# When four scatter accumulators are zeroed: a graph-network layer on one Trainium2 core

## The chip, the cores and the metric

The kernel runs on one core of one Trainium2 chip. The metric is the time of one execution on the device in microseconds (us). The kernel before takes 2061.96 us, the median of three runs (2057.36 to 2062.47).

A core has five engines that this text names as the profile does: PE (matrix products; PEld is its weight load), DVE (vector work), ACT (activations and copies), POOL and SP. SP does no arithmetic here: it issues almost all the plain transfers, in program order, and an entry in its queue that waits for a semaphore holds up every entry behind it. POOL issues the indirect transfers (the scatters).

## The reference, cut to what matters

A graph has 6250 nodes with 128 features and 200000 edges. Every edge takes the row of its `dst` node, multiplies it by a filter worked out from 20 edge attributes, and the result is added to the row of its `src` node.

```python
h = relu(layernorm(x))
v = h @ W_in
W_ij = (softplus(f_ij @ W_f1 + b_f1) - log 2) @ W_f2 + b_f2
W_ij = W_ij * f_ij_cutoff
x_ij = v[dst] * W_ij
out  = segment_sum(x_ij, src, num_segments=6250)
y    = x + (softplus(out @ W_o1 + b_o1) - log 2) @ W_o2 + b_o2
```

The edges are sorted by `dst`; `src` is in no order. The segment sum over `src` is the part that this change touches.

## The kernel before, in words

**Tiling.** 128 edges are a chunk, four chunks a quad; 391 quads. A loop over items `i` (L1208) works on several quads at once: in item `i`, PE makes the first product of quad `i+1` (`s1_pe`, L313), gathers and filters quad `i-1` (`s2_pe_x`, `s2_pe_w`), DVE multiplies the two (`s2_m`, L520), and so on. In the middle of the run an item takes a little under 5 us. What stands beside this skeleton is hung into it by `at(item, point, function, ...)`; `run(i, point)` calls it. The point "L" is the first of an item, right behind the loads of two coming quads (`load_sc`, in even items, for the quads four and five ahead). Nothing is reordered afterwards: each engine runs its instructions in the order in which the functions are called.

**Two ways for the segment sum.** 168 of the quads (`mpq`, from quad 8 on, every second or third one) are permuted on chip and summed by PE into `accT`, an SBUF tile of 128 x 6272 numbers. The other 223 quads (`splain`) are scattered by POOL: `scatter` (L579) adds 128 rows of 512 bytes to an accumulator in DRAM, one instruction per chunk. Rows that overflow on the first way are scattered as well (`os`, `oji` in the profile). In all there are 987 scatters.

**Accumulators.** An addition to a row reads it and writes it back, so two scatters that may touch the same rows must not be under way together: a scatter waits until the last one into the same accumulator has landed. There are four accumulators of 6400 rows (`ACC_R`), `acc0` to `acc3`, and `acc_of` (L566) picks one by the scatter's number `k`: `acc0` alone up to `K1_END`, `k % 2` up to `K2_END`, `k % 3` up to `K3_END`, then `k % 4`, and near the end the last three. Each has to be zeroed before its first use, by ten pieces (`zero_piece`, L164) of 320 KB that copy a zeroed stretch `zero` of `accT` into DRAM. POOL issues the pieces of `acc0` and `acc1` in the first 40 us, SP those of `acc2` (items `Z2`) and `acc3` (items `Z3`).

**Lists.** Within a chunk, edges with the same `src` must be summed before the scatter. 31 of the scattered quads do this on PE (`s3_pe`; the index tile is `ji`). The other 192, quads 12 to 203 of `splain`, form 12 windows of 16 quads: one edge of each chunk and node goes to the node's row, duplicates go to rows of a list behind the 6400 rows (index tile `lji`, worked out by `l_eq` to `l_index` during the window before, from `sb` loads two items earlier). The list of window `w` has 128 rows from `l_base(w)` on, and later windows have lower ones: a scatter of window `w` is allowed the rows up to `l_base(w) + 128`, its own list and those of the later windows. When a window is done, `l_load` (`lm` in the profile) reads its 128 list rows from the four accumulators and they are added to their nodes. The list rows of all windows, 1536 in each accumulator, are zeroed by three pieces of 256 KB per accumulator (`zero_list`, L170), in items 1 to 12.

**Buffers.** The data of a scatter lies in one of four `s` buffers per quad, which comes free when the scatters that read it have landed. The index tile `oji` has two buffers.

Of the kernel before, what the change touches and what calls it, by code (L numbers as in the profile page):

```python
# [7 lines left out]
F32 = mybir.dt.float32  # L8
# [12 lines left out]
P = 128  # L21
# [13 lines left out]
SW = 16  # L35
# [19 lines left out]
def tile_gnn(ctx: ExitStack, tc: tile.TileContext, x, fB, cT, srcT, srcr, dstr, win_, wf1, wf2, bias, bo1c, wo1,  # L55
             wo2, consts, ident, cmap, out, n_edges):
    nc = tc.nc
    N = out.shape[0]
    NP = x.shape[0]
# [15 lines left out]
    ACC_R = NP + P  # L75
    GN = NP // GRP
    ZR = 10 if ACC_R % 10 == 0 else 1
    ZL = 3
    K1_END, K2_END, K3_END = 2, 8, 140
    Z2, Z3 = [0,0,1,1,2,2,3,3,4,4], [5+2*j for j in range(10)]  # L80
    mpq = sorted_quads(NQ)
    mpi = {q: n for n, q in enumerate(mpq)}
    units = unit_its(mpq)
    splain = [q for q in range(NQ) if q not in mpi]
    plain = {q: n for n, q in enumerate(splain)}
    NS = len(splain)
    LB, LE = listed(NS) if spread else (0, 0)
# [6 lines left out]
    NW = (LE - LB) // SW  # L94
    LR = P * NW
# [8 lines left out]
    cp = ctx.enter_context(tc.tile_pool(name="cp", bufs=1))  # L104
# [7 lines left out]
    accs = []  # L112
# [25 lines left out]
    wo1_sb = cp.tile([P, P], F32, name="wo1_sb")  # L138
    wo2_sb = cp.tile([P, P], F32, name="wo2_sb")
    accT = cp.tile([P, NP], F32, name="accT")  # L140
    zero = accT[:, :ACC_R // ZR]
    wgtb = cp.tile([P, 1], BF16, name="wgtb")
    iotw = cp.tile([P, GN // 2 + SLOTS], F16, name="iot")
    iot = iotw[:, GN // 2:]
# [22 lines left out]
        for h in range(parts):  # L167
            eng.dma_start(v[j][:, h * w:(h + 1) * w], zero[:, :w])

    def zero_list(k, j):  # L170
        v = accs[k][ACC_R:].rearrange("(p t) f -> p (t f)", p=P)
        w = LR // ZL
        nc.sync.dma_start(v[:, j * w:(j + 1) * w], zero[:, :w])

    def xt_load(g):
        o, T = groups[g]
# [186 lines left out]
    def l_base(w):  # L363
        return ACC_R + P * (NW - 1 - w)
# [470 lines left out]

    with tc.manual_schedule():
        nc.scalar.preload_act_table_set("natural_log_exp_and_others")
        nc.gpsimd.memset(zero, 0.0)
        for j in range(ZR * 4 // 10):
            zero_piece(nc.gpsimd, 0, j)  # L840
# [108 lines left out]
        def at(i, point, fn, *a):  # L949
            hooks.setdefault((i, point), []).append((fn, a))  # L950
# [6 lines left out]
        if CE < EP // P:  # L957
            w = (CE + 4 * NS) // 2
# [128 lines left out]
        if spread:  # L1087
            k = clear(mid + 9, busy, 2)
# [3 lines left out]
            k = clear(NQ - 1, busy, 2)  # L1092
# [21 lines left out]
        for r in range(-(-len(mpq) // RKQ)):  # L1114
            i = mpq[RKQ * r]
            at(i - 5, "D2", rank_group, r)
            k = clear(i - 4, units)
            at(k, "PE2", rank_count, r)
            at(k + 1, "D0", rank_own, r)
            k = clear(k + 1, units)  # L1120
# [5 lines left out]
        for w in range((LE - LB) // SW):  # L1126
# [25 lines left out]
            k = clear(i + 1, units)  # L1152
# [5 lines left out]
            at(k + 2, "S", over_scatter, ("L", w))  # L1158
        if LE:
            for k in range(NACC):  # L1160
                for j in range(ZL):
                    at((0, 3, 6, 9)[k] + j + 1, "L", zero_list, k, j)
        for q in mpq:
            at(q + 1, "D2", perm_oh, q)
            at(q + 2, "D2", part_rem, q, 1)
# [17 lines left out]
            if mpi[q] % 2 or q == mpq[-1]:  # L1183
                at(q + 5, "DM", over_idx, q)
                at(q + 6, "A0", over_dg, q)
                k = clear(q + 6, units)
                at(k, "PE2", over_row, q)
                at(k + 1, "D0", over_eq, q)
                k = clear(q + 8, units)
# [259 lines left out]
def sorted_quads(nq):  # L1449
    qs, q = [], MP0  # L1450
    while q < nq - MPEND:
        qs.append(q)
        q += MPGAPS[(len(qs) - 1) % len(MPGAPS)]
    return qs if len(qs) % RND <= EXTRA else qs[:len(qs) // RND * RND]
# [14 lines left out]
def listed(ns):  # L1469
    k = (ns - LEARLY - LLATE) // SW  # L1470
    b = (ns - LLATE - SW * k) // 4 * 4
    return b, b + SW * k
# [6 lines left out]
def clear(i, busy, n=1):  # L1479
    while any(i + k in busy for k in range(n)):  # L1480
        i += 1
    return i
# [113 lines left out]
```

## Time and profile before

| | |
|---|---|
| median of three runs | 2061.96 us |
| the profiled execution, time | 2079.2 us |
| the profiled execution, span of its instructions | 2077.4 us |
| mean granted clock of PE | 0.963 |
| bytes moved by DMA | 272.57 MB, mean 131 GB/s |
| scatters on POOL | 987, mean 1.62 us |

Times in the profile's rows are us from the start of the span. A timeline row has the start, the duration, the engine (with a "q" for an instruction that only issues a transfer), the source line, the operation, "out<-in" by the program's names, the shape, "xcount" for rows merged, and in brackets the idle time of the engine before it and what ended it. "DMA acc<-s,ji" as what ended it means the landing of a scatter. A row of the groups has "busy us, mean ns" behind the first bar and "idle us" with its releasers behind the second. A row of the waits reads: who waited, for whom, us in total, times, longest.

### The profile page before, as it was taken

The numbers are of one execution on the slowest core, as the hardware profiler recorded it, in microseconds if no ns is written. First come the engines' busy times: TensorE is split into PE (matmuls) and PEld (weight loads), VectorE is DVE, ScalarE is ACT, GpSimd is POOL, SyncE is SP. The second block draws the span as 40 slices with busy tenths as digits, with TensorE's granted clock in tenths as the row PEclk, the third lists the DMA queues.
The fourth block names the chain that finished last, engine by engine and source line by source line (L and its number), as shares of the span: only waits on it lengthen the run. The fifth ranks groups of instructions, "written<-read, shape, count | busy, mean of one in ns | idle before, by whom it ended". The sixth has DMA issues, their size and how long they took to land. (4 is left out here: it accounts for less than half of the span.)

```text
span 2077.4 us, 57578 instructions
## 1 busy us (share of the span) xinstructions
PE 1862.5 (90%) x20381; PEld 1288.0 (62%) x20381; DVE 1659.4 (80%) x4448; ACT 1482.8 (71%) x4083; POOL 1643.9 (79%) x1040
## 2 busy tenths in 40 slices
PE   3579988899999999999999999999999999999956
PEld 2456666566666666666666666666666666677734
DVE  3678887797888888988988978979889788787635
ACT  2468776777776777777678777777877777788714
POOL 3578787888877888887878878888888888888774
PEclk9679999999999999999999999999999999999977
DMA  7887766667766766766667666676676676667648
GB/s 238 227 210 147 125 118 120 121 112 130 130 118 114 126 127 119 139 123 123 120 120 130 120 119 118 118 124 117 120 134 108 124 121 111 110 119 131 130 48 239
DMA packets 381188, 272.57 MB, mean 131 GB/s; under 512 B 97727, under 2 KB 341354, under 8 KB 380898
## 3 DMA queue, kind: packets, MB, share of 16 engines
q0 software_dynamic: 143728, 71.30, 35.2%
q1 hardware_dynamic: 236882, 197.50, 34.1%
q8 instruction: 161, 2.64, 0.5%
q14 instruction: 129, 1.06, 0.2%
q10 hardware_dynamic: 288, 0.07, 0.0%
HBM read 154.45 MB, written 114.24 MB: 129 GB/s over the span
## 5 line engine op out<-in xcount | busy, mean ns | idle before, releaser
L582 POOL DMA_INDIRECT acc<-s,lji x768 | 1245.7, 1622 | 266.6 <-issue 180.3
L687 PE MATMUL pq<-pt,pm 128*128 128x387 bf16 x2688 | 533.0, 341 | 44.6 <-DVE pt L676 10.6
L510 ACT ACTIVATE xc<-xg,cb 128x128 f32<-128x128 f32 x1564 | 446.4, 371 | 135.7 <-PE xg L497 119.9
L505 PE MATMUL W<-w,a 128*128 128x128 f32 x3128 | 464.1, 292 | 0.1
L505 PEld LDWEIGHTS W<-w,a 128*128 128x128 f32 x3128 | 388.4, 195 | 42.3 <-issue 3.1
L687 PEld LDWEIGHTS <-pm 128*128 128x128 bf16 x2688 | 260.3, 99 | 233.4 <-issue 37.2
L693 ACT CAST mst<-pq 128x387 bf16<-128x387 f32 x672 | 302.2, 481 | 135.0 <-PE pq L687 96.5
L781 PE MATMUL un<-so,mst 32*128 32x392 bf16 x8064 | 374.5, 327 | 17.3 <-DVE pr L627 7.0
L781 PEld LDWEIGHTS <-mst 32*128 32x128 bf16 x8064 | 227.8, 93 | 157.1 <-issue 60.2
L323 ACT ACTIVATE a<-a,con 128x512 f32<-128x512 f32 x391 | 282.3, 722 | 12.7
L582 POOL DMA_INDIRECT acc<-s,ji x123 | 200.2, 1628 | 80.4 <-issue 26.4
L318 ACT ACTIVATE a<-z 128x512 f32<-128x512 f32 x391 | 238.3, 610 | 26.8 <-PE z L313 17.2
L676 DVE TENSOR_TENSOR pt<-pt 128x512 f32<-128x512 f32 x336 | 231.8, 690 | 5.8
L662 DVE TENSOR_SCALAR pm<-iot,pos 128x576 bf16<-128x576 f16 x672 | 221.8, 391 | 0.0
L792 DVE TENSOR_TENSOR accT<-un,accT 128x392 f32<-128x392 f32 x320 | 158.6, 558 | 73.7 <-PE un L781 37.5
L520 DVE TENSOR_TENSOR s<-W,xc 128x512 f32<-128x512 f32 x192 | 131.9, 687 | 85.9 <-ACT xc L510 52.0
L766 DVE TENSOR_SCALAR so<-iot,mst 128x392 bf16<-128x392 f16 x672 | 191.0, 344 | 6.7 <-PE un L781 6.7
L582 POOL DMA_INDIRECT acc<-os,oji x96 | 156.4, 1629 | 31.2 <-issue 18.0
L497 PE MATMUL xg<-wn,oh 63*128 63x128 bf16 x1564 | 157.3, 222 | 15.8 <-ACT xc L510 9.4
L313 PE MATMUL z<-ft,ws 123*128 123x512 bf16 x391 | 152.0, 389 | 15.7 <-DVE iotl L941 9.4
L494 PE MATMUL W<-b2rep,onesb 64*128 64x512 bf16 x391 | 153.9, 394 | 0.0
L520 DVE TENSOR_TENSOR pt<-W,xc 128x512 f32<-128x512 f32 x168 | 115.2, 686 | 47.9 <-ACT xc L510 29.5
(209 smaller groups left out, 2435.5 us busy)
## 6 DMA issues: line engine op xcount, KB each, us to landing
rb<-reld SPq DMA_DIRECT2D x391, 64.0 KB
fsd<-f SPq DMA_DIRECT2D x49, 480.0 KB
ft<-fsd SPq DMA_DIRECT2D x195, 120.0 KB
sb<-src SPq DMA_DIRECT2D x169, 128.0 KB
fb<-in_fB_dram SPq DMA_DIRECT2D x49, 320.0 KB
ft<-fsd SPq DMA_DIRECT2D x195, 80.0 KB
wn<-tab SPq DMA_DIRECT2D x782, 15.8 KB
acc<-s,lji POOLq DMA_INDIRECT x768
```

The costliest lines, as they stand in the source:

```text
L318: nc.scalar.activation(a, st[q]["z"], AF.Exp)
L323: nc.scalar.activation(a, a, AF.Ln, bias=half, scale=0.5)
L505: nc.tensor.matmul(W[:, c, :], st[q]["a"][:, c * P:(c + 1) * P], w2, start=False, stop=(c == 3))
L510: nc.scalar.mul(xc[:, c, :], st[q]["xg"][:, c, :], late["c", q // CQ][:, 4 * (q % CQ) + c:4 * (q % CQ) + c + 1])
L520: nc.vector.tensor_tensor(m[:, :, :P], st[q]["W"], st[q]["xc"], op=ALU.mult)
L582: nc.gpsimd.indirect_dma_start(out=accs[k][:rows, :], out_offset=bass.IndirectOffsetOnAxis(ap=ji, axis=0), in_=s, in_offset=None, compute_ ...
L662: nc.vector.tensor_scalar(pm[:, c], iot[:, :SLOTS], rk[r]["pos"][:, 4 * j + c:4 * j + c + 1], None, op0=ALU.is_equal)
L676: nc.vector.tensor_tensor(pt[:, :, k * P:(k + 1) * P], a, high(a), op=ALU.subtract)
L687: nc.tensor.matmul(t[:, :PW], mp[q]["pm"][:, c, s * P:(s + 1) * P], high(mp[q]["pt"][:, c:c + 1, :PW])[:, 0], start=(c == 0), stop=(c == 3))
L693: nc.scalar.copy(mp[q]["ms", s][:, :PW], mp[q].pop(("q", s))[:, :PW])
L766: nc.vector.tensor_scalar(so, iotw[:, :GN], w[:, 3 * P // 2:3 * P // 2 + 1], None, op0=ALU.is_equal)
L781: nc.tensor.matmul(ts[g][:, :GN], mp[q]["ms", s][v, k * P:(k + 1) * P], mp[q]["oh"][v], start=(q == qs[0] and k == 0), stop=(q == qs[-1] a ...
```

## The change

The third accumulator comes into use with scatter 40 (before: 8); it is zeroed in items 6 to 15 (before: 0 to 4), the fourth in items 20 to 38, every second one (before: 5 to 23, every second one). The tile `zero` moves to the last 640 columns of `accT`. The list rows are zeroed by 48 pieces of 64 KB (128 rows of 512 bytes, one per window and accumulator) out of a zeroed tile `zl` of its own; the four of a window stand 8, 6, 4 and 2 items ahead of the window's first quad. The descriptor space of POOL's transfers is set to 8192 bytes of a partition (before: the default, 16384). The instructions of PE, DVE and ACT and their order are the same as before; POOL has one memset more, SP 36 transfers more.

```diff
-    ZL = 3
-    K1_END, K2_END, K3_END = 2, 8, 140
-    Z2, Z3 = [0,0,1,1,2,2,3,3,4,4], [5+2*j for j in range(10)]
+    K1_END, K2_END, K3_END = 2, 40, 140
+    Z2, Z3 = [6 + j for j in range(10)], [20 + 2 * j for j in range(10)]
...
-    zero = accT[:, :ACC_R // ZR]
+    zero = accT[:, NP - ACC_R // ZR:]
+    zl = cp.tile([P, P], F32, name="zl")
...
-    def zero_list(k, j):
-        v = accs[k][ACC_R:].rearrange("(p t) f -> p (t f)", p=P)
-        w = LR // ZL
-        nc.sync.dma_start(v[:, j * w:(j + 1) * w], zero[:, :w])
+    def zero_list(k, w):
+        o = l_base(w)
+        nc.sync.dma_start(accs[k][o:o + P, :], zl)
...
+        nc.gpsimd.memset(zl, 0.0)
         nc.gpsimd.memset(zero, 0.0)
...
         if LE:
             for k in range(NACC):
-                for j in range(ZL):
-                    at((0, 3, 6, 9)[k] + j + 1, "L", zero_list, k, j)
+                for w in range(NW):
+                    at(max(1, splain[LB + SW * w] - 8 + 2 * k), "L", zero_list, k, w)
...
-    nc = bacc.Bacc("TRN2", target_bir_lowering=False, num_devices=1)
+    nc = bacc.Bacc("TRN2", target_bir_lowering=False, num_devices=1, dynamic_dma_scratch_size=8192)
```

## The prediction

> **What bounds the kernel now.** I read the page first, for the busy shares, the slices and the chain of waits; then the groups of POOL by stretch of time, its timeline, the waits, and last SP's, DVE's and ACT's timelines around the places where the new transfers will stand.
>
> ```profile
> PE 1862.5 (90%) x20381; PEld 1288.0 (62%) x20381; DVE 1659.4 (80%) x4448; ACT 1482.8 (71%) x4083; POOL 1643.9 (79%) x1040
> ...
> PE   3579988899999999999999999999999999999956
> ...
> GB/s 238 227 210 147 125 118 120 121 112 130 130 118 114 126 127 119 139 123 123 120 120 130 120 119 118 118 124 117 120 134 108 124 121 111 110 119 131 130 48 239
> ...
> PE 31%; DVE 6%; ACT 3%; DMA 3%; issue 2%; POOL 2%; SPq 1%; DVEq 0%; POOLq 0%; ACTq 0%
> ```
>
> A slice is 52 us. PE is full from the seventh slice on, and the chain, which reaches back over the second half of the span, runs mostly through PE. The first three slices are different: PE at 3, 5 and 7 tenths while DMA moves 210 to 238 GB/s, nearly twice the later 120. The next rows group POOL's scatters in three stretches (busy us, mean ns, then idle us and what ended it): 81 to 156, 156 to 376 and 1400 to 1800 us.
>
> ```profile
> L582 POOL DMA_INDIRECT acc<-s,ji x33 | 57.3, 1736 | 20.3 <-DMA acc<-s,ji 10.4 <-issue 5.4 <-ACT a L323 2.7
> ...
> L582 POOL DMA_INDIRECT acc<-s,lji x94 | 150.3, 1599 | 34.7 <-issue 20.4 <-DMA acc<-s,lji 7.2 <-DVE eql L369 1.6
> ...
> L582 POOL DMA_INDIRECT acc<-s,lji x187 | 302.9, 1620 | 57.0 <-issue 45.5 <-DMA acc<-s,lji 4.3 <-DVE accT L792 1.2
> ```
>
> A scatter costs POOL 1.6 to 1.7 us and about 0.3 us of issue. From 81 us on POOL hardly rests: (57.3+20.3)/33 = 2.35 us a scatter in the first stretch, with half of the idle time spent on the landing of an earlier scatter into the same accumulator, and (150.3+34.7)/94 = 1.97 us in the second. That POOL sets the pace of PE's side there, and not the other way, is seen in who waits for its landings:
>
> ```profile
> ACT s L540 <- DMA acc<-s,ji: 6.1, 3, 3.3
> ...
> 368.41 0.29 ACT L755 ACTIVATE oji<-ojd,con 128x1 int32<-128x1 f32 x1 [14.47 <-DMA acc<-os,oji]
> ```
>
> The first row (waits, 80 to 170 us) is ACT kept from refilling the four `s` buffers, the second is ACT standing 14.47 us until POOL had worked off its backlog. So a delay of POOL before 376 us is passed on whole: ACT resumes when POOL has caught up. Behind that, PE sets the pace.
>
> **The change, part by part.** The sum is made against the profiled execution's own 2079.2 us (span 2077.4), which is 17 above the median of the runs, 2061.96; I carry the difference over to that median.
>
> *Scatters 8 to 39 on two accumulators instead of three.* A scatter may start when the last one into its accumulator has landed. While `K2_END` was not reached, the trace already has two in use:
>
> ```profile
> 55.36 1.78 POOL L582 DMA_INDIRECT acc<-s,ji  x1 [18.73 <-ACT ji L563]
> 59.14 1.57 POOL L582 DMA_INDIRECT acc<-s,ji  x1 [2.00 <-DMA acc<-s,ji]
> 66.92 1.54 POOL L582 DMA_INDIRECT acc<-s,ji  x1 [6.21 <-DMA acc<-s,ji]
> ...
> 72.41 1.54 POOL L582 DMA_INDIRECT acc<-s,ji  x1 [2.04 <-DMA acc<-s,ji]
> ...
> 76.58 1.54 POOL L582 DMA_INDIRECT acc<-s,ji  x1 [0.30 <-DMA acc<-s,ji]
> ...
> 83.10 1.54 POOL L582 DMA_INDIRECT acc<-s,ji  x1 [0.65 <-DMA acc<-s,ji]
> ```
>
> All six go into accumulator 0, so the distances are start to restart: 3.78, 7.78, 5.49, 4.17, and 6.52 us once three are in use. With two accumulators the distance from scatter to scatter is half a restart, or 1.85 if that is more. I take 5.4 us, near the middle row: 2.7 us a scatter against 2.35, over 32 scatters +11. The ends are 2.1 (restart 4.2, -8) and 3.5 (restart 7, +37). That the restarts stay long has a reason in the change: zeroing is mostly moved within this stretch. Items 6 to 15 now issue ten pieces of the third accumulator (ten of 320 KB); before, six of the fourth's pieces and eight list pieces of 256 KB stood in items 5 to 15, about 4 MB against 3.5.
>
> The Trainium skill, "DMA: Bandwidth & Descriptors", section "Queues, rings and completion order", says that each DMA engine takes turns between the queues at packet granularity; by it a scatter's landing stretches whenever SP's queue has packets, so equal bytes would mean equal restarts. The trace bears it out as far as the row 66.92, with its wait of 6.21 us, lies where DMA moves 227 GB/s.
>
> *Items 0 to 5 lose their zeroing.* Ten pieces of the third accumulator and four list pieces, 4.3 MB, leave the stretch from 46 to 77 us. DVE's wait in the next row is for a load that stood in SP's queue behind such pieces:
>
> ```profile
> 46.30 0.97 SPq L168 DMA_DIRECT2D acc<-accT  x2
> 47.31 0.45 SPq L344 DMA_DIRECT2D sb<-src  x1
> ...
> 83.62 1.23 DVE L369 TENSOR_TENSOR eql<-sb,srcT_sb 128x1024 bf16<-128x1024 int16 x1 [8.76 <-DMA sb<-src]
> ```
>
> PE's side may come out of this up to 8.76 us earlier, but POOL is the bound, and for it only scatters 0 to 7 come sooner: between 0 and 6 us (the wait before 66.92), I take 3. Early part together: +8.
>
> *List pieces that wait.* Formerly all list rows were zeroed before any list scatter. Now the pieces of window w >= 1 are issued 8, 6, 4 and 2 items ahead of it, while scatters of window w-1 run, whose allowed rows include them. So each of 44 pieces waits on SP for the last list scatter into its accumulator, and the next one waits for the piece. Behind it in SP's queue stand the loads of the next items and the `sb` loads that DVE needs one or two items later. The price depends on how far POOL trails. Window 1, item 37 (SP, then POOL, then DVE):
>
> ```profile
> 243.00 3.06 SPq L295 DMA_DIRECT2D ft<-fsd  x3
> ...
> 250.13 0.84 SPq L344 DMA_DIRECT2D sb<-src  x2
> ...
> 259.10 2.14 POOL L582 DMA_INDIRECT acc<-s,lji  x1 [2.06 <-DMA acc<-s,lji]
> ...
> 256.56 1.21 DVE L369 TENSOR_TENSOR eql<-sb,srcT_sb 128x1024 bf16<-128x1024 int16 x1
> ```
>
> The piece stands ahead of 243.00 and must wait for the scatter of 259.10 to land, some 4 us later (3.78 was the shortest restart, 1.85x3 = 5.6 the turn that three accumulators allow). SP goes on at 263; it issues the item's loads and `sb` by 271 (7.1 us, as 243.00 to 250.13), landed at 274: DVE loses 17 us. POOL trails by about as much there, and the 14.47 us that ACT loses at 354 to 368 go away with its lead, so +3 (0 to 8).
>
> Window 11, item 325, has no such cover later:
>
> ```profile
> 1663.96 2.23 SPq L295 DMA_DIRECT2D ft<-fsd  x3
> ...
> 1670.69 1.79 SPq L344 DMA_DIRECT2D sb<-src  x4
> ...
> 1674.65 1.80 POOL L582 DMA_INDIRECT acc<-s,lji  x1 [0.31 <-issue]
> ...
> 1678.77 1.21 DVE L369 TENSOR_TENSOR eql<-sb,srcT_sb 128x1024 bf16<-128x1024 int16 x1
> ```
>
> Release at 1678.7, `sb` landed near 1688: 9 us on PE's path, of which POOL's backlog lets me count +8 (4 to 9). In window 6 (item 181) the same sum gives +3:
>
> ```profile
> 967.67 1.16 SPq L295 DMA_DIRECT2D ft<-fsd  x3
> ...
> 971.59 1.54 POOL L582 DMA_INDIRECT acc<-s,lji  x1 [0.30 <-issue]
> ...
> 974.01 0.85 SPq L344 DMA_DIRECT2D sb<-src  x2
> ...
> 981.36 1.21 DVE L369 TENSOR_TENSOR eql<-sb,srcT_sb 128x1024 bf16<-128x1024 int16 x1
> ```
>
> Release 975.6, `sb` issued 982 and landed at 984.5. In the other windows the scatter in question lands within a few us of SP's turn: 0 each, at most 5.
>
> *POOL behind the pieces.* A piece has the size of the lm loads, whose four issues at 778.6 to 779.9 us feed PE at 783.1:
>
> ```profile
> L469 PEld LDWEIGHTS lsum<-lm,leq x8: 192/192/192, 783.1 to 783.9; 128*128 128x128 f32 x8
> ...
> L451 SPq DMA_DIRECT2D lm<-acc x4: 355/380/382, 778.6 to 779.9; - x4
> ```
>
> 3.2 us after a landing at 4 makes 7.2. Three accumulators come round in 5.6 us (window 1: 1.6 each, twice), four in 7.4 (0 unless late). +2 (0 to 10).
>
> The Trainium skill, same page, section "Rules for kernel authors", advises to coalesce small transfers, since under 64 KB one pays mostly overhead; 48 pieces for 12 goes against it. On the estimate of 2 us fixed (that page, "Anatomy of one DMA") 36 more would cost 72 us if they stood one after the other on the path. The trace has the 3.2 us, but SP's queue runs ahead of its users, so I count only what is waited for.
>
> *The rest at nothing.* POOL's extra memset is a fifth of the one of `zero`; the zero tile at the end of `accT` is written only in item 42, after the last piece of item 38. The descriptor space is halved; if POOL had to wait for room, its scatters would last longer, and they keep a shortest time of 1.54 us in crowded and calm rows alike. Bound: the mean's excess, 1.62-1.54, over 987 scatters is 80 us, doubled at worst +80; I take 0.
>
> Sum: 8+3+8+3+2 = +24, 2103 in a profile, 2086 by the median; I say 2085.
>
> **The rivals.**
>
> *Faster: the landings get short.* If, with items 0 to 5 unloaded, a restart is 3.7 us or less, two accumulators cost nothing: 32 scatters at 2.05 instead of 2.35, -10, 3 earlier, and with a smaller backlog only half of the SP stalls, +7: 2056. For it: 3.78 and 4.17 do occur. Against: 5.49 to 7.78 too, at the same traffic that the change keeps in items 6 to 15. It decides below a restart of 3.7.
>
> *No change.* Restart 4.6 (2.3 a scatter, -2, and 3 earlier), and the late `sb` loads are absorbed by POOL's backlog in window 11 as in window 1: 2062. Against it: the chain is PE's there.
>
> *Much slower.* Restarts of 7 us all through (+37, 3 earlier), SP stalls +16: 2112. For it: 7.78 and 6.52. Against it: 2.35 x 3 = 7.05 is the most that three accumulators in turn allow, and only a third of those scatters waited.
>
> *The halved descriptor space makes POOL slower*, which isn't what the change is about: +80, 2142. Nothing shows it.
>
> **How the numbers follow.** Forecast 0.55 (its own range 2070 to 2100), faster 0.14, no change 0.11, much slower 0.16, descriptor space 0.04. The time is the forecast's, 2085. The range, 2058 to 2112, leaves out half of the faster case, the last one and the far half of the much slower one. A measurement here tells 0.3%, 6 us, from no change: slower 0.53+0.16+0.04+0.02 = 0.75, same 0.12, faster 0.13.
>
> **What would show it.** In the stretch of scatters 8 to 39: about 2.7 us each, with the landing of an earlier scatter as main releaser; below 2.2 the early term is wrong. At items 37 and 325: SP waiting some 15 to 20 us in the new list line, and DVE's `eql` waiting for `sb` right behind; if `eql` doesn't wait, those terms are wrong. ACT's 14.47 us before `oji` shrinks or goes. POOL's mean scatter stays near 1.62 us; if it grows, it was the descriptor space. A kernel whose first 156 us are shorter by 10 would overturn the forecast.

## The result, and the profile after

The changed kernel takes 2097.97 us (median of 5 runs, 2095.76 to 2100.06) where the kernel before takes 2062.47 (5 runs): the ratio is 1.0172, with the interval 1.0155 to 1.019. It is 35.5 us slower.

The page of the changed kernel begins with the busy shares, two rows of the 40 slices (52 us each) and the chain.

```profile
span 2095.7 us, 57684 instructions
PE 1863.1 (89%) x20381; PEld 1289.1 (62%) x20381; DVE 1655.6 (79%) x4448; ACT 1488.5 (71%) x4083; POOL 1629.0 (78%) x1041
...
PE   3578959999999999999899999999998989999956
...
GB/s 233 181 153 136 139 112 129 131 134 111 132 127 115 133 120 132 135 124 114 121 135 125 115 133 124 120 123 122 130 109 127 127 114 107 118 117 125 133 45 241
...
SPq 1%; DMA 1%; PE 0%; DVE 0%; ACT 0%; POOL 0%; issue 0%; DVEq 0%; POOLq 0%
```

PE is busy for 1863.1 us, where the two profiles of before (the second is that of experiment 1) have 1862.5 and 1855.9, so of the 35 us some 28 are idle time, and up to 7 may be slower work. The mean granted clock of PE is 0.957, against 0.963 and 0.965; from 200 to 300 us, where PE stands, it is 0.88 against 0.98 and 0.97. No run separates the clock from the waits. Slice 6 (262 to 314 us) has PE at 5 tenths where it had 8. The third slice moves 153 GB/s where it moved 210: the unloading of the start did happen. The chain reaches back over the end of the span only, so I read the groups and timelines. POOL's scatters, in the three stretches that the prediction used (busy us, mean ns, then idle us and what ended it):

```profile
L581 POOL DMA_INDIRECT acc<-s,ji x27 | 43.4, 1608 | 32.3 <-DMA acc<-s,ji 25.3 <-issue 6.6 <-ACT h L223 0.3
...
L581 POOL DMA_INDIRECT acc<-s,lji x89 | 142.4, 1600 | 36.1 <-issue 23.0 <-DMA acc<-s,lji 6.9 <-DVE s L519 1.3
...
L581 POOL DMA_INDIRECT acc<-s,lji x186 | 299.0, 1608 | 61.5 <-issue 43.0 <-DMA acc<-zl 5.4 <-DMA acc<-s,lji 4.6
```

From 81 to 156 us a scatter now takes (43.4+32.3)/27 = 2.80 us, and 25.3 of the 32.3 idle us end with the landing of an earlier scatter. A scatter itself costs POOL 1.61 us at 1400 to 1800 us, as before. How the early loss reaches PE's side is seen in ACT, which fills the `s` buffers that the landings free. These are its waits over the whole span, in the changed kernel and then in the second profile of before:

```profile
ACT s L539 <- DMA acc<-s,ji: 47.7, 8, 10.9
...
ACT s L540 <- DMA acc<-s,ji: 9.7, 2, 8.3
```

Then the two places that the prediction named. Item 37 (SP, then DVE and PE, and ACT's next `oji` behind):

```profile
253.16 0.46 SPq L264 DMA_DIRECT2D fb<-in_fB_dram  x1
273.37 0.32 SPq L172 DMA_DIRECT2D acc<-zl  x1
273.78 1.16 SPq L294 DMA_DIRECT2D ft<-fsd  x3
...
279.38 0.93 SPq L343 DMA_DIRECT2D sb<-src  x2
...
284.16 1.23 DVE L368 TENSOR_TENSOR eql<-sb,srcT_sb 128x1024 bf16<-128x1024 int16 x1 [17.90 <-DMA sb<-src]
285.31 0.69 DVE L519 TENSOR_TENSOR pt<-W,xc 128x512 f32<-128x512 f32 x1
...
286.05 0.58 PE L312 MATMUL z<-ft,ws 123*128 123x512 bf16 x1 [15.87 <-DMA ft<-fsd]
...
378.06 0.29 ACT L754 ACTIVATE oji<-ojd,con 128x1 int32<-128x1 f32 x1
```

SP issues nothing between 253.6 and 273.4, because the list piece waits; the `sb` loads stand behind it and `eql` loses 17.90 us. PE stands 15.87 us there. The row names a load of `ft` as what ended it, but that load was issued from 273.78 on, and `z` starts just as DVE's product behind `eql` ends (285.31 + 0.69 = 286.00); by the code, `z` takes the PSUM buffer that this product frees. So I read PE's wait as that of `eql`. The 14.47 us that ACT lost in front of `oji` are gone. Item 325:

```profile
1688.92 0.35 SPq L172 DMA_DIRECT2D acc<-zl  x1
1689.37 1.18 SPq L294 DMA_DIRECT2D ft<-fsd  x3
...
1694.65 3.19 SPq L343 DMA_DIRECT2D sb<-src  x4
...
1698.63 1.25 DVE L368 TENSOR_TENSOR eql<-sb,srcT_sb 128x1024 bf16<-128x1024 int16 x1 [7.88 <-DMA sb<-src]
```

The waits over the whole span (us, times, longest) put a number on the new line:

```profile
SPq L172 <- DMA acc<-s,lji: 126.4, 30, 19.7
...
DVE eql L368 <- DMA sb<-src: 37.8, 7, 17.9
...
POOL acc L581 <- DMA acc<-zl: 16.4, 20, 3.0
```

### The profile page after: what moved, and what is told of

Read it like the earlier page. It is cut to its first block, busy times and chain, and to the rows that moved or that the text cites. A ratio compares the mean times of both kernels' runs of the same rounds, so it can differ in the third digit from the quotient of the medians.

```text
span 2095.7 us, 57684 instructions
## 1 busy us (share of the span) xinstructions
PE 1863.1 (89%) x20381; PEld 1289.1 (62%) x20381; DVE 1655.6 (79%) x4448; ACT 1488.5 (71%) x4083; POOL 1629.0 (78%) x1041
## 5 line engine op out<-in xcount | busy, mean ns | idle before, releaser
L780 PE MATMUL un<-so,mst 32*128 32x392 bf16 x8064 | 381.4, 333 | 22.0 <-DVE pr L626 12.9
L581 POOL DMA_INDIRECT acc<-s,ji x123 | 196.0, 1593 | 96.7 <-DMA acc<-s,ji 36.8
L312 PE MATMUL z<-ft,ws 123*128 123x512 bf16 x391 | 152.0, 389 | 38.5 <-DMA ft<-fsd 30.9
L581 POOL DMA_INDIRECT acc<-os,oji x96 | 155.2, 1616 | 31.2 <-issue 16.5
L496 PE MATMUL xg<-wn,oh 63*128 63x128 bf16 x1564 | 157.1, 222 | 14.5 <-ACT xc L509 11.9
L368 DVE TENSOR_TENSOR eql<-sb,srcT_sb 128x1024 bf16<-128x1024 int16 x96 | 117.0, 1219 | 42.1 <-DMA sb<-src 37.8
```

The lines of the kernel that those rows point to most:

```text
L581: nc.gpsimd.indirect_dma_start(out=accs[k][:rows, :], out_offset=bass.IndirectOffsetOnAxis(ap=ji, axis=0), in_=s, in_offset=None, compute_ ...
L780: nc.tensor.matmul(ts[g][:, :GN], mp[q]["ms", s][v, k * P:(k + 1) * P], mp[q]["oh"][v], start=(q == qs[0] and k == 0), stop=(q == qs[-1] a ...
```

## The experiments

The kernels below ran in four groups, each on another chip beside runs of the kernel before. These had medians of 2064.21, 2071.45, 2075.35 and 2072.88 us from group to group, so kernels are compared by their ratios. Of each of them there is one profile.

**1. The kernel before, once more.** Its first profiled execution took 2079.2 us, 17 more than its median, while that of the changed kernel (2097.45) is typical. Between these two profiles there are only 18 us.

> The kernel before once more, for a second profile. The two profiles differ by 18.3 us in span, the medians by 35.5: the profiled execution of before (2079.2) was 17 above its own median. Theory A, its early part was unlucky: this profile shows a span near 2060, and ACT's 14.47 us at oji (354 to 368 us) is shorter or gone. Theory B, the 17 us lie spread over the run: a span near 2060 with the same stall of 14 us. Theory C, 2079 is as frequent as 2062: a span of 2077 again.

It took 2062.76, span 2061.0. ACT's wait in front of `oji` is there all the same:

```profile
365.86 0.29 ACT L755 ACTIVATE oji<-ojd,con 128x1 int32<-128x1 f32 x1 [14.99 <-DMA acc<-os,oji]
```

So the stall belongs to the kernel and not to one slow execution, and the 17 us are spread over the run. Below, "before" in a trace is this second profile.

**2 and 3. The two halves of the change.** The lists alone (48 pieces, with the zero tile moved and the descriptor space halved):

```
     K1_END, K2_END, K3_END = 2, 8, 140
     Z2, Z3 = [0,0,1,1,2,2,3,3,4,4], [5+2*j for j in range(10)]
...
+    def zero_list(k, w):
+        o = l_base(w)
+        nc.sync.dma_start(accs[k][o:o + P, :], zl)
```

> The 48 list pieces alone (with zl, the moved zero tile and the smaller descriptor space); accumulators and their zeroing as before. Theory of the forecast (SP waits on scatters, and eql waits for sb behind it, in windows 1, 6 and 11): 17 us at window 1, partly covered, 5 at window 6, 9 at window 11: +20 to +30 by the medians, 2082 to 2092, and some 100 us of SP waiting in the list line. Rival, two accumulators are the whole loss: not over +4, 2066.

And the accumulators alone, with 12 list pieces where they were before:

```
+    K1_END, K2_END, K3_END = 2, 40, 140
+    Z2, Z3 = [6 + j for j in range(10)], [20 + 2 * j for j in range(10)]
+    zero = accT[:, NP - ACC_R // ZR:]
```

> The later use and later zeroing of the third and fourth accumulator alone; lists zeroed by 12 pieces in items 1 to 12 as before. Theory of the forecast: scatter 40 starts 8 to 10 us later than before (165 instead of 156 us) and the end shifts by that: 2068 to 2074. Rival, the list waits are the whole loss: 2060 to 2064, with scatter 40 at 156 or sooner. Without the list pieces' relief in items 1 to 5 the scatters may come later still, 170 us.

Lists alone: 2082.69, ratio 1.0093 [1.0057, 1.0128]. Accumulators alone: 2082.0, 1.0092 [1.0059, 1.0125]. The halves add up within their intervals: 0.93% and 0.92% against 1.72%. The lists alone came out as expected in time. The accumulators alone cost 18 us where 4 to 10 were expected (2068 to 2074), and scatter 40 starts at 172.39 us, where 165 or at worst 170 was expected. Where each half arises is seen when the start of DVE's product (`s2_m`), for which PE's side must have a quad's data ready, is compared with the same quad in before (us later than before, worked out from the traces):

```
time before   lists alone   accumulators alone   changed kernel
   188            -3.0            +20.9              +11.7
   262           +12.8            +20.1              +30.8
   352           +12.4            +19.9              +30.1
   405            -0.5            +19.7              +17.1
   550            +1.0            +17.9              +19.3
   939            +1.7            +15.7              +19.8
  1085            +6.1            +17.0              +24.2
  1556           +10.5            +19.3              +24.9
  1658           +18.7            +22.2              +27.9
  1795           +21.5            +21.1              +36.0
```

The accumulators' part is lost before 188 us and stays. The lists' part comes in steps: 16 us at item 37, most of it given back by 405 us when ACT's stall disappears, 4 near 1000 (item 181), and 11 between 1556 and 1795 us. Of these 11, item 325 is 3, with SP standing 7.2 us there; in the changed kernel SP stands 12.9 us and it costs 8. The halves do not add up stage by stage: early on the changed kernel loses 12 us, not the 21 of the accumulators alone; the lists alone gain 3 there, which covers a part of the difference. The first profile of before, compared in the same way, drifts to 16 us by 1658 us, by up to 6 between two rows, so a single small step of one trace proves little.

**4. The descriptor space alone.**

```
-    nc = bacc.Bacc("TRN2", target_bir_lowering=False, num_devices=1)
+    nc = bacc.Bacc("TRN2", target_bir_lowering=False, num_devices=1, dynamic_dma_scratch_size=8192)
```

> The kernel before with 8192 bytes of descriptor space instead of 16384, nothing else. Forecast's reading: no change, 2059 to 2066, a mean scatter of 1.62 us on POOL. Rival, the halved space explains what the two profiles leave open: +17, 2079, and a mean scatter above 1.64 us.

2065.16, ratio 1.0005 [0.9988, 1.0022]: it costs nothing.

**5 to 7. Is it the waiting of SP, or the number of pieces?** First, all 48 pieces early, where they have nothing to wait for:

```
-                    at(max(1, splain[LB + SW * w] - 8 + 2 * k), "L", zero_list, k, w)
+                    at(4 + w, "L", zero_list, k, w)
```

> The changed kernel with its 48 list pieces issued four at a time in items 4 to 15, before any list scatter, so that no piece has a scatter to wait for; all else as changed. Theory A (SP stands behind list pieces that wait for a scatter, and the sb loads behind them come late): the whole price of the lists goes and only that of the accumulators is left, 2082 us (2077 to 2087), no eql row of 10 us or more in windows 1, 6 and 11, and ACT's wait of about 15 us for oji comes back. Theory B (48 small transfers cost by their number, wherever they stand): 2095 us or more.

2087.38, ratio 1.0065 [1.0043, 1.0087], the price of the accumulators alone or less (early on its trace loses 13 us, as the changed kernel does, not 21). The waits of this kernel:

```profile
ACT oji L754 <- DMA acc<-os,oji: 17.5, 3, 14.5
...
DVE eql L368 <- DMA sb<-src: 13.0, 5, 6.2
```

No row of SP waiting in the list line is left; `eql` has lost its long wait, and ACT's stall at `oji` is back. Theory A holds: 36 transfers more cost nothing that can be measured. By the Trainium skill, "DMA: Bandwidth & Descriptors", section "Rules for kernel authors", small transfers should be coalesced; the runs bear no price out here (1.0065 with 48 pieces, 1.0092 with 12), and the 72 us of the prediction's estimate did not come. The Trainium skill gives the 2 us of that estimate, on the same page in "Anatomy of one DMA", for transfers that POOL issues; SP issues these. That the 36 more cost nothing because SP's queue runs ahead of what it feeds is my reading.

Then the pieces later, behind the `sb` loads:

```
-                    at(max(1, splain[LB + SW * w] - 8 + 2 * k), "L", zero_list, k, w)
+                    at(max(1, splain[LB + SW * w] - 5 + k), "L", zero_list, k, w)
```

> The changed kernel with each list piece issued 5, 4, 3 and 2 items ahead of its window instead of 8, 6, 4 and 2, so that it stands behind the sb loads that serve the window's start; the pieces are as many and still wait for the scatter before. Theory A (what costs is that eql gets its sb late): eql's waits in windows 1, 6 and 11 go, 2084 us (2079 to 2089), though SP still waits 50 us or more in the list line. Theory B (the wait of SP costs wherever it stands, because ft and other loads behind it come late too): 2094 us or more, with new waits of PE for ft. A later piece may also meet its scatter late, which would show as POOL waiting longer for zl than 16 us in sum.

2105.36 (2098.51 to 2114.55), ratio 1.0145 [1.0118, 1.0172]. The time is Theory B's, but its sign is missing: PE does not wait more for `ft`,

```profile
PE z L312 <- DMA ft<-fsd: 18.2, 3, 9.1
```

(30.9 us in the changed kernel, by the same view of the waits, with the 15.9 of item 37 in it). What the expectation named as a third way did come: POOL waits longer for the pieces, 28.8 us where it was 16.4, and SP stands 142.3 us where it was 126.4.

```profile
POOL acc L581 <- DMA acc<-zl: 28.8, 20, 4.6
```

The rest is seen in SP's, POOL's and DVE's timelines of this kernel:

```profile
1003.23 10.48 SPq L172 DMA_DIRECT2D acc<-zl  x2
...
1022.39 1.71 POOL L581 DMA_INDIRECT acc<-s,lji  x1 [10.67 <-DVE pt L675]
...
1598.45 0.35 SPq L172 DMA_DIRECT2D acc<-zl  x1
...
1604.13 1.77 SPq L343 DMA_DIRECT2D sb<-src  x4
1607.88 1.23 DVE L368 TENSOR_TENSOR eql<-sb,srcT_sb 128x1024 bf16<-128x1024 int16 x1 [7.41 <-DMA sb<-src]
```

The long waits of `eql` at items 37 and 325 went, but a piece now stands in front of another window's `sb` loads (1598 to 1608), and at 1012 to 1022 POOL loses 10.67 us while the window's pieces are still being issued. (The row names a DVE result as releaser; that it was a piece is my inference and was not tried.) The stand was moved, not removed.

So the last of the three takes the stand away only at the three places that were given a price:

```
-                    at(max(1, splain[LB + SW * w] - 8 + 2 * k), "L", zero_list, k, w)
+                    i0 = {1: 4, 6: 8, 11: 12}.get(w)
+                    at(max(1, splain[LB + SW * w] - 8 + 2 * k) if i0 is None else i0 + k, "L", zero_list, k, w)
```

> The changed kernel with the 12 list pieces of windows 1, 6 and 11 alone issued in items 4 to 15, where they wait for nothing; the other 36 stay where the change puts them and still hold SP up. Theory A (only where SP's stand reaches eql does it cost, and that is in these three windows): the ratio to the kernel before falls from 1.0172 to that of the accumulators alone, 1.0065 to 1.0095, with SP still waiting 70 us or more in the list line. Theory B (every stand of SP costs a little): in proportion to the pieces moved, 1.013 or more.

Ratio 1.0095 [1.0068, 1.0122] (2092.16 us): the accumulators' price, at the upper edge of what Theory A gave. The waits of this kernel:

```profile
SPq L172 <- DMA acc<-s,lji: 65.5, 20, 8.0
...
DVE eql L368 <- DMA sb<-src: 7.9, 4, 3.3
...
ACT oji L754 <- DMA acc<-os,oji: 14.0, 1, 14.0
```

SP still stands 65.5 us at the other 36 pieces (70 or more were expected), and `eql` feels little of it: 7.9 us, no wait over 3.3. Against the kernel with all pieces early (1.0065) there is room for some us from these pieces, but the two intervals overlap. The traces show one place for them, window 10. Right behind its waits (7.5 and 5.0 us in the changed kernel), between 1555 and 1599 us, DVE's product falls back by 4.0 us in the changed kernel, 4.7 with the lists alone and 4.3 in this kernel. In the first profile of before and the seven other kernels whose list pieces do not wait, the same stretch changes by 0.7 at most. `eql` waits only 2.2 to 3.2 us there; what else PE's side waits for stays open.

**8. Two accumulators and nothing else.** All zeroing as before:

```
-    K1_END, K2_END, K3_END = 2, 8, 140
+    K1_END, K2_END, K3_END = 2, 40, 140
```

> The kernel before with one number changed: the third accumulator comes into use at scatter 40 instead of 8; all zeroing stays where it was. Theory A (two accumulators set the pace through the landing of the scatter before): scatters 8 to 39 take 2.7 to 3 us each, the time is 2080 us (2074 to 2086), as with the whole accumulator part. Theory C (what stretches the landings is the zeroing moved into items 6 to 15): scatters 8 to 39 stay near 2.4 us, 2066 us (2060 to 2072).

2093.77, ratio 1.0101 [1.0079, 1.0123], the whole price of the accumulator part. POOL's group from 81 to 156 us, in this kernel:

```profile
L582 POOL DMA_INDIRECT acc<-s,ji x27 | 42.5, 1575 | 36.0 <-DMA acc<-s,ji 31.9 <-issue 3.9 <-ACT mst L693 0.3
```

(42.5+36.0)/27 = 2.91 us a scatter. So the long distances between scatters need no moving of the zeroing: here all of it stands where it was.

**9. The unloading alone.** Three accumulators from scatter 8, but the fourth zeroed in items 20 to 38 and the 12 list pieces in items 5 to 16:

```
+    Z2, Z3 = [0,0,1,1,2,2,3,3,4,4], [20 + 2 * j for j in range(10)]
...
+                    at((0, 3, 6, 9)[k] + j + 5, "L", zero_list, k, j)
```

> The kernel before with the fourth accumulator zeroed in items 20 to 38 instead of 5 to 23, and the 12 list pieces (256 KB each) in items 5 to 16 instead of 1 to 12; three accumulators from scatter 8 on, as before. It takes the part of the change that unloads the start and leaves its two prices out. If landings early on are stretched by SP's transfers: scatters 8 to 39 fall from 2.35 to about 2.15 us each and the time is 2056 us (2052 to 2060). If POOL's own issue sets the pace there: 2064 us (2060 to 2068).

2073.95, ratio 1.0012 [0.9995, 1.0028]: nothing. PE's side had its data up to 7.5 us earlier (at 148 us), POOL did not: scatters 8 to 39 at 2.28 us each, scatter 40 at 151.56 us where it was 151.90.

**10 and 11. The opposite of the change.** If zeroing at the start is free and accumulators save waits, the fourth should come sooner:

```
+    K1_END, K2_END, K3_END = 2, 8, 40
+    Z2, Z3 = [0,0,1,1,2,2,3,3,4,4], [5+j for j in range(10)]
```

> The kernel before turned the other way: the fourth accumulator zeroed in items 5 to 14 and in use from scatter 40 instead of 140. Theory A (in the early stretch POOL waits for landings of 4 to 5 us, and the more accumulators, the fewer such waits; the zeroing that stands there costs nothing): scatters 40 to 139 go from 2.01 to 1.93 us each, that is 8 us earlier at scatter 140, ACT's wait of 15 us for oji is shorter by as much, and the time is 0.3% shorter (2054 to 2062 where the kernel before takes 2064). Rival (the pace there is POOL's own issue, and what it gains is lost again behind PE): no change within 0.2%.

```
+    K1_END, K2_END, K3_END = 2, 8, 16
+    Z2, Z3 = [0,0,1,1,2,2,3,3,4,4], [3,3,4,4,5,5,6,6,7,7]
```

> As the last, but the fourth accumulator is zeroed two pieces an item in items 3 to 7 and in use from scatter 16. Theory A: scatters 8 to 39 go from 2.24 to about 2.0 us each (8 us) and scatters 40 to 139 to 1.93 (8 us more), until no backlog keeps ACT waiting for oji; of these 16 us what PE can use, 8 to 14: 2050 to 2056 where the kernel before takes 2064. Rival (3.2 MB more in front of scatter 16 stretch the first loads and landings): first scatter or its neighbours later by 5 us and the time 2062 to 2070.

From scatter 40: 2073.16 where before took 2075.35, ratio 0.9981 [0.9966, 0.9996]. That is short of the 0.3% expected and inside the 0.2% of its rival, so the time does not decide; the trace has scatters 40 to 139 at 1.95 us (1.93 expected, 2.01 before) and a longest wait at `oji` of 6.5 us instead of 15. From scatter 16: 2068.1, ratio 0.9962 [0.9943, 0.9981], faster than both kernels of this study. POOL's group from 81 to 156 us, in the second profile of before,

```profile
L582 POOL DMA_INDIRECT acc<-s,ji x35 | 56.8, 1624 | 21.4 <-DMA acc<-s,ji 14.5 <-issue 5.5 <-DMA sb<-src 1.0
```

and in the kernel with the fourth from scatter 16:

```profile
L582 POOL DMA_INDIRECT acc<-s,ji x35 | 57.5, 1644 | 20.4 <-issue 10.2 <-DMA acc<-s,ji 7.7 <-ACT s L540 1.1
```

The wait of ACT in the latter, over its whole span:

```profile
ACT oji L755 <- DMA acc<-os,oji: 2.6, 1, 2.6
```

The landings' share of the idle time is 7.7 us where it was 14.5 (35 scatters in each), issue takes up half of that, and the stall at `oji` is 2.6 instead of 15 us. Scatters 8 to 39 take 2.19 us each, not the 2.0 expected, 40 to 139 take 1.95 (2.01 before); the gain, 0.4%, is at the low end of what was expected.

## Why the prediction was right, and where its sizes were off

The direction and the three places were right. The forecast was +23 against 35.5 measured. By the table above (changed kernel, last column), the 36 us of the trace are, rounded: 17 up to 405 us, of which POOL's early part is 13 and item 37 the other 4; 2 by 550; 4 at item 181; 4 from there to 1658, about where window 10 stands; 8 at item 325.

*Scatters 8 to 39 on two accumulators*: a restart of 5.4 us was taken; scatter 8 starts at 76.71 and scatter 40 at 164.97, 2.76 us each, a restart of 5.5. What was mis-sized is the other side of the subtraction. 2.35 came from the one profile at hand; the second has 2.24 between scatters 8 and 40 (80.13 to 151.90), and the kernels that use three accumulators from scatter 8 to 39 lie between 2.22 and 2.41. Over 32 scatters that is +16.5, not +11. The reason given for long restarts, that the change keeps the zeroing traffic in the stretch, is not borne out. Experiment 8 has them with nothing moved, and experiment 5, whose early pieces bring the zeroing issued between scatters 8 and 40 to 5760 KB where the changed kernel has 3136, takes 2.74 us a scatter against 2.76.

*Items 0 to 5 lose their zeroing*: -3 was taken; scatter 8 starts 3.4 us sooner than in the second profile of before (76.71 against 80.13). Right. With the row above, the early part is +13 where +8 stood. Against the first profile, from which the sum was made, it is +9 (164.97 against 155.95): most of the error lies in the base. Part of this is luck. The accumulators alone lose 20 us there, 2.90 us a scatter (experiment 3), and the lists that leave the start give back 7, where the sum has +11 and -3 for all of it; why the lists matter so much was not tried.

*Item 37*: SP's wait of 15 to 20 us and DVE's 17 were predicted; 19.7 and 17.90 came, the stall at `oji` went, and the net is +4 against +3. *Item 325*: +8 predicted, 8 measured, with `eql` waiting 7.88. *Item 181*: +3 predicted, some 4 measured, with `eql` waiting 4.0. Experiment 7 shows that these three carry most of the list part: without their stands, the ratio is that of the accumulators, at the upper edge.

*The other windows at nothing*: in the changed kernel's trace some 6 us arise there (2 by 550, 4 from 1085 to 1658). The first are no larger than what two executions differ by. Window 10 is not at nothing: some 4 us, in each of three kernels with the late pieces, which is inside the "at most 5" of the prediction.

*POOL behind the pieces, +2*: POOL waited 16.4 us for `zl`, never over 3.0. At the places where PE sets the pace this has no visible step. *The rest at nothing*: experiment 4 shows it for the descriptor space; the move of the zero tile is inside experiment 9, which cost nothing; the extra memset is inside experiment 2 and was not measured by itself.

*Carrying the 17 us of the profiled execution over to the median* was right: experiment 1 shows them spread over the run, with the stall at `oji` in place. A comparison of the first two profiles alone would have shown half of the loss.

Of the rivals, *faster* needed a restart of 3.7 or less; 5.5 came. *No change* needed `sb` at item 325 to be absorbed; it wasn't. *Much slower* needed restarts of 7. *The descriptor space* fell with experiment 4.

## What to carry to other kernels

A transfer that waits holds up what stands behind it in its queue, so look there for its cost: 20 waits of SP, 65.5 us together, cost a few us at most, and those at three places cost 0.8%, with one engine's next input queued behind them. Length and place are not fully told apart, for two of the three were also the longest waits (19.7 and 12.9 us; no other over 8.0). The nearest to a test is item 181: 7.3 us of waiting cost some 4 us there, and 7.8 us in front of 558.7 us (window 3) cost less than 1. Where a stage is paced by the landing of the write before it, count how many targets take turns, and spend free bandwidth early on one more. Size a difference from two profiles of the same kernel where you can: of the 5 us by which the early part was sized too small, 4 are the difference between two profiles of before.

## What the runs showed of the hardware

In one stretch the landings were shorter where DMA had less to move. It is the one from 54 to 66 us (length, POOL busy, TensorE clock, DMA share, GB/s), first in the second profile of before:

```profile
54.00:66.00 12.00, 3.62 (x3) 0.72 0.84 230
```

and then in the changed kernel:

```profile
54.00:66.00 12.00, 5.57 (x4) 0.72 0.69 178
```

The three scatters that start in this stretch take 4.8 us, in the mean, from start to the end of their last packet in the one and 3.0 in the other. That agrees with the Trainium skill, "DMA: Bandwidth & Descriptors", section "Queues, rings and completion order", by which each DMA engine takes turns between queues at packet granularity. Three scatters do not make it a rule: the one before them in the changed kernel, at 52.98 us, took 4.8 us as well, most of it within the same stretch. Nor did the lower share last: from 78 to 102 us the changed kernel is at 0.83 to 0.88, as the rows say,

```profile
78.00:90.00 12.00, 5.01 (x5) 0.76 0.83 186
90.00:102.00 12.00, 7.41 (x5) 0.64 0.88 191
```

and of the 3.8 MB that SP and POOL issue there, 0.6 MB are the moved zeroing itself and the rest mostly loads. That this is why taking transfers out of the start bought nothing in experiment 9 is a guess, which no run tests.
